# One kernel, a list order played in advance: a new account of DMAs, two weights loaded later, one more group turned, a longer finishing period

## The chip, the cores and the metric

The kernel runs on one core of a Trainium2 chip. Its time is the device time of one execution in microseconds (us); smaller is better. Three executions of the kernel before gave 932.15, 932.08 and 930.09 us, so the median is 932.08 us.

A core has five engines that take their own lists of instructions in order: TensorE (PE, matmuls; its weight loads are shown apart as PEld), VectorE (DVE), ScalarE (ACT), GpSimd (POOL) and SyncE (SP). In this kernel nearly every DMA is issued by SP. An instruction waits at the head of its list until the semaphores that it needs have come; what stands behind it waits too.

## The reference, cut to what matters

Four layers run one after the other on x of shape (8, 512, 256), all in float32. The first is a transformer block with a bias on the attention scores; it has nearly all the work.

```
x   = ln(src) * (1 + scale) + shift                 # scale, shift from an embedding of the step
q, k, v = x @ Wq + bq, x @ Wk + bk, x @ Wv + bv     # 16 heads of 16
scores  = q @ k.T / 4 + attention_bias              # bias: (8, 16, 512, 512) float32
scores  = where(mask, -inf, scores)
x   = x + softmax(scores) @ v @ Wo + bo
x   = x + gelu2((ln(x) * g2 + beta2) @ W1 + b1) @ W2 + b2   # 256 -> 1024 -> 256
x   = adapter(x, expert of the batch entry)         # 256 -> 64 -> 64 -> 256, residual, layer norm
x   = rotate(x, theta, phi)                         # pairs of columns
x   = adapter(x, expert of the batch entry)         # second set of weights
```

The bias is 128 MB and is read once. Everything else is small beside it.

## The kernel before, in words

**Units.** The attention is cut into 128 units. A unit is one batch entry, one group of four heads and one tile of 128 queries: it needs four bias tiles of 128x512, 256 KB each. Sixteen units make one batch entry. Within a batch entry the order is half (two query tiles), group, query tile; so eight units make one half.

**One unit (`attention`, L880 and after).** SP loads the four bias tiles (L898) into four of the 16 slots `BIAS`. POOL adds the mask, 0 or -1e30, to each (L902). PE makes the scores of four heads, which lie side by side in the rows of the array (L910; eight matmuls in the trace for one unit). DVE forms the negated sum of scores and bias and the minimum of each row (L922). ACT takes the exponential, less the row's maximum (L926). Then the 128x512 probabilities must be transposed for the product with v, and there are two ways:

- by PE: four transposes of 128x128 (L961) into one bank of PSUM, and one copy out by ACT or DVE (L682 in the profile, in the helper `evict`);
- "turned": DVE transposes 32x32 blocks (`nc.vector.transpose`, L937), and four DMAs issued by SP place the blocks (L946, pT<-tb). PE does nothing.

Where a group is turned, two of its four heads (`TURNED = 2`) take the second way. `turned_groups` (L361) says which groups: in the first batch entry only the last group, in the last batch entry all but the last group, in the others all four. For every second unit PE multiplies the probabilities of two query tiles with v (L987), transposes the result back (L1005), and DVE normalises it.

**Everything else.** `prepare(b)` makes normalised x, q, k and v of a batch entry, with its own loads of x and mask and of a broadcast modulation row (mod, L871), which waits until the kernel itself has written `ada_rows` (L486). `finish(b, ts)` does all that comes after attention for one half (two query tiles): the output product (L748), the feed-forward (L1043 into 1024 columns, L1052, L1055 and L1059 for the activation, L1068 back), two adapters (L1085, L1098, L748) and the rotation. `experts_matrices` fetches for each batch entry two small matrices chosen by an index that SP first reads from memory (L1210, then two DMAs at L1214). `late_weights` loads w1 and w2, 1024 KB each (L565, L567), and smaller ones.

**The order.** Nothing of this is written in the order in which it runs. Each piece is a `Task` with a cost, an engine, what it reads and writes, and a rank. `Plan.run` (L142) plays the list as a simulation on the host: whenever an engine is free it takes, among the tasks whose inputs are there and whose buffers are free, the one of the lowest rank. The order that comes out is the order in which instructions are emitted, and so the order of every engine's own list. The costs have no other effect; the chip runs the lists at its own pace. A DMA task costs SP its issue time; its data are taken to be there when a single counter, `queues`, has advanced by the task's `data`, plus 2.4 us. Any number of DMAs may be under way, and the counter starts at zero.

The ranks say how urgent a task is in units: bias loads of unit n have rank n - 2, the pieces of `finish` after unit n are spread by their PE cost from n + 2 to n + 11, for n from 110 on to n + 19 (L1278). For the last half the two query tiles are finished apart.

Of the kernel before, what the change touches and what calls it, by code (L numbers as in the profile page):

```python
# [20 lines left out]
B, S, D, H, HD, FF = 8, 512, 256, 16, 16, 1024  # L21
# [48 lines left out]


class Task:
    def __init__(self, costs, emit, rank, mode, at, data):
        self.costs, self.emit, self.rank, self.data = costs, emit, rank, data
        self.engine = None
        self.mode, self.at = mode, at
        self.waits, self.then, self.buffers = 0, [], []


class Plan:  # L80

    AFTER = {PE: 0.22, DVE: 0.14, ACT: 0.16, POOL: 0.12, DMA: 2.4}

    def __init__(self):
        self.tasks, self.written, self.read = [], {}, {}
        self.rank, self.stream = 0.0, None

    def __call__(self, engine, cost, emit, r=(), w=(), mode=None, at=0.0, data=0.0):  # L90


        if isinstance(engine, dict):
            task = Task(engine, emit, self.rank, mode, at, data)
        else:
            task = Task({engine: cost}, lambda e: emit(), self.rank, mode, at, data)
# [47 lines left out]
    def run(self, free_at):  # L144
        ready = {e: [] for e in free_at}
        mode = dict.fromkeys(free_at)
        events, order, seq = [], [], 0
        for n, t in enumerate(self.tasks):
            t.n = n
            if t.waits == 0:  # L150
                heapq.heappush(events, (t.at, seq, "ready", t))
                seq += 1
        for e, at in free_at.items():
            heapq.heappush(events, (at, seq, "free", e))
            seq += 1
        idle = set()
        now, queues = 0.0, 0.0
        while events:
            now, _, what, x = heapq.heappop(events)
            if what == "ready":  # L160
                for e in x.costs:

                    later = 1.0 if e == DVE and ACT in x.costs else 0.0
                    heapq.heappush(ready[e], (x.rank + later, x.n, x))
            elif what == "free":
                idle.add(x)
            elif what == "over":
                for b in x.buffers:
                    b.left -= 1
                    if b.left == 0:  # L170
                        b.home.free.append(b.slot)
            if events and events[0][0] == now:
                continue
            for e in [e for e in free_at if e in idle]:
                held, short = [], set()
                while ready[e]:
                    entry = heapq.heappop(ready[e])
                    t = entry[2]
                    if t.engine is not None:
                        continue  # L180
                    new = [b for b in t.buffers if b.slot is None]
                    wanted = {}
                    for b in new:
                        wanted[b.slots] = wanted.get(b.slots, 0) + 1
                    lacking = [
                        s for s, n in wanted.items()
                        if len(s.free) + (
                            len(s.lender.free) if s.lender and s.lender not in short else 0
                        ) < n
                    ]  # L190
                    if not lacking:
# [12 lines left out]
                if t.mode is not None and t.mode != mode[e]:  # L204
                    cost += 1.3 if e == ACT else 0.1
                    mode[e] = t.mode
                idle.discard(e)
                t.start, t.end = now, now + cost
                order.append(t)
                heapq.heappush(events, (t.end, seq, "free", e))  # L210
                seen = t.end
                if e == DMA:
                    queues = max(queues, now) + t.data
                    seen = max(seen, queues)
                seen += self.AFTER[e]
# [14 lines left out]
def conditioned_sequence_kernel(  # L230
# [129 lines left out]

    def turned_groups(b):  # L361

        return 3 if b == 0 else 0, NG - 1 if b == B - 1 else NG

    def rows_of(t, r, n):
        return t[:, r : r + 1, :].to_broadcast([P, n, D])
# [184 lines left out]
    def late_weights():  # L551
        wo_rows = w_o.rearrange("(c m e) n -> m e c n", c=NC, e=32)

        def load(rank, cost, data, emit, key):
            plan.rank = rank
            plan(DMA, cost, emit, [], [key], data=data)

        load(-1.5, 0.45, 0.8, lambda: nc.sync.dma_start(
            wv, w_v.rearrange("(c p) n -> p c n", p=P)), "wv")
# [1 line left out]
            bv_row, rows_in[R_BV * D : (R_BV + 1) * D].partition_broadcast(P)), "bv")  # L561
        load(2.5, 1.0, 1.0, lambda: [
            nc.sync.dma_start(wo[:, c], wo_rows[:, :HD, c]) for c in range(NC)
        ], "wo")
        load(1.1, 0.45, 3.0, lambda: nc.sync.dma_start(  # L565
            w1, w_1.rearrange("(c p) n -> p c n", p=P)), "w1")
        load(1.2, 0.45, 3.0, lambda: nc.sync.dma_start(  # L567
            w2, w_2.rearrange("(c p) n -> p c n", p=P)), "w2")
        load(2.6, 0.5, 0.5, lambda: nc.sync.dma_start(
            wd, down_w.rearrange("l (c p) a -> p l c a", p=P)), "wd")  # L570
# [4 lines left out]
    def rotations():  # L575
# [14 lines left out]
                )  # L590
            nc.sync.dma_start(cc.t[B : B + 1], rows_in[None, R_B2 * D : (R_B2 + 1) * D])

        plan(DMA, 1.0, load, [], [gb, (cc, "b2")], data=0.2)
        plan.rank = 2.5
        four = "p (g u v) -> p g u v"

# [26 lines left out]
        def store():  # L623
# [1 line left out]
            nc.sync.dma_start(turned_rows, cc.t[:B])  # L625

        plan(DMA, 0.7, store, [*((ab, u, v) for u in range(2) for v in (None, 0, 1)), (cc, "c")],
             ["rot_rows", "turned_rows"], data=0.2)

        def bias_rows():  # L630

# [7 lines left out]
            nc.sync.dma_start(wu[A1:K1, 1], turned_rows)  # L639

        plan.rank = 6.8
        plan(DMA, 1.6, bias_rows, ["turned_rows"], ["wu"], data=0.6)
        plan.rank = 7.0
        ps = Buffer(BG, lambda t: t[:, : NC * (B + 1)].rearrange("p (c b) -> p c b", c=NC))

# [112 lines left out]
    def prepare(b):  # L758
# [99 lines left out]
        plan(DMA, 1.8, turned_values, [(v_pad, t) for t in range(NT)], [v_turn], data=1.0)  # L858
# [29 lines left out]
    def attention(u, n):  # L888
# [60 lines left out]

        if turned:  # L950
            plan(DMA, 2.5, moved, [(tb, j) for j in range(turned)], [(pT, i)],
                 data=1.05 * TURNED)
        plan.rank = n + 0.0

        whole = "p (j k i q c) -> p j k i q c"
# [230 lines left out]
    def experts_matrices():  # L1186
# [19 lines left out]
        for b in range(B):  # L1206
            plan.rank = 2.7 + 0.55 * b

            def fetch(b=b):
                e = nc.sync.value_load(  # L1210
                    expert_i[:, b : b + 1], min_val=0, max_val=E - 1,
                )
                for l in range(2):
                    nc.sync.dma_start(  # L1214
                        raw.t[:, l, b, :],
                        experts[l].rearrange("(e p) a -> e p a", e=E)[bass.ds(e, 1)].rearrange(
                            "o p a -> (o p) a"),
                    )

            plan(DMA, 2.0, fetch, ["expert"], [(raw, b)], data=0.2)  # L1220

        def kept():
            nc.gpsimd.tensor_tensor(
# [43 lines left out]
    for n, u in enumerate(units):  # L1267
# [115 lines left out]
```

## Time and profile before

| | |
|---|---|
| three executions | 930.09 to 932.15 us, median 932.08 us |
| the profiled execution | 929.78 us |
| its span, first to last instruction | 927.8 us |
| PE busy | 893.6 us, 96% of the span |
| DVE, ACT, POOL busy | 788.3, 752.7, 754.0 us (85%, 81%, 81%) |
| DMA, mean over the core's 16 engines | 73.7% of the span for SP's queue; 216.48 MB at 233 GB/s |
| bias loads (L898) | 512 of 256 KB |
| transposes by PE (L961) | 1152 |
| block transposes by DVE (L937), DMAs that place them (L946) | 224, 448 |

How to read it. Busy time says how long an engine had an instruction in it. For PE this contains waiting inside the pipeline, so 96% does not mean that PE runs at its peak. More is told by the chain of waits (what released each step of the work that ended last) and by the busy times of each stretch of 25 us, because the kernel has a start, a long even middle and an end, and each has another limit. Where the profile puts an idle time down to "DMA bias<-in_bias", a bias tile had not landed. The granted clock of PE (1.00 is full speed) stands in the table of stretches too.

### The profile page before, as it was taken

To read this page: it belongs to the slowest core of one execution; us is meant where nothing else is said; L and a number is where in the kernel's file an instruction comes from. 1 tells how busy PE (TensorE), PEld (TensorE's weight loads), DVE (VectorE), ACT (ScalarE), POOL (GpSimd) and SP (SyncE) were. 2 spreads that over 40 slices of the span, in tenths; PEclk is the share of its full clock that TensorE was granted. 3 is DMA by queue.
4 is the path that set the end of the run, shared out by engine and by line. 5 is a ranking of instruction groups with operands and counts; after the bars stand their busy time and mean duration, and the time that the engine had idled before them with its cause. 6 is when DMAs were issued, how large, how long until landed. Compare 5 with 4: busy or idle time off the path is not lost.

```text
span 927.8 us, 21009 instructions
## 1 busy us (share of the span) xinstructions
PE 893.6 (96%) x6654; PEld 591.8 (64%) x6654; DVE 788.3 (85%) x2152; ACT 752.7 (81%) x1387; POOL 754.0 (81%) x843
## 2 busy tenths in 40 slices
PE   9989999999999999999999999999999999899994
PEld 7545766566666666667666666666666676566783
DVE  4557888988988989889998889989899899999666
ACT  5957869969898889969799697987989697998553
POOL 7589899987998878978798887989789788989132
PEclk9989999999999999999999999999999999999997
DMA  9578487787977879796966979877895978978000
GB/s 318 192 240 280 151 285 230 215 285 208 300 231 233 262 235 301 203 292 216 315 216 215 303 223 281 261 247 243 251 289 164 288 229 275 288 235 270 18 24 24
DMA packets 160913, 216.48 MB, mean 233 GB/s; under 512 B 18911, under 2 KB 91657, under 8 KB 160802
## 3 DMA queue, kind: packets, MB, share of 16 engines
q1 hardware_dynamic: 160758, 215.12, 73.7%
q8 instruction: 53, 0.87, 0.4%
q14 instruction: 58, 0.48, 0.2%
q10 hardware_dynamic: 44, 0.02, 0.0%
HBM read 149.89 MB, written 4.24 MB: 166 GB/s over the span
## 4 chain that ended last, share of the span: by engine, by line
PE 59%; ACT 10%; DMA 10%; DVE 9%; POOL 6%; issue 4%; SPq 2%; POOLq 0%; DVEq 0%; ACTq 0%
PE bank L910 10%; PE bank L1068 9%; PE bank L961 9%; PE bank L1043 9%; PE bank L987 8%; PE bank L748 4%; DMA bias<-in_bias 4%; PE bank L800 4%; POOL bias L902 3%; ACT bias L926 3%; DMA pT<-tb 2%; DVE bias L922 2%; PE bank L724 2%; ACT pT L682 2%; PE bank L838 1%
## 5 line engine op out<-in xcount | busy, mean ns | idle before, releaser
L902 POOL TENSOR_TENSOR bias<-bias,neg 128x512 f32<-128x512 f32 x512 | 580.1, 1161 | 81.6 <-DMA bias<-in_bias 63.7
L926 ACT ACTIVATE bias<-bias,low 128x512 f32<-128x512 f32 x512 | 344.8, 722 | 62.0 <-DVE low L922 61.2
L922 DVE CUSTOM_DVE_ANT_0 bias<-bank,bias 128x512 f32<-128x512 f32 x512 | 329.7, 684 | 48.3 <-PE bank L910 35.2
L961 PEld LDWEIGHTS bank<-shifted,bias 128*128 128x128 f32 x1152 | 129.0, 142 | 57.1 <-issue 21.6
L961 PE MATMUL bank<-shifted,bias 128*128 128x128 f32 x1152 | 159.3, 279 | 4.5 <-ACT pT L682 2.3
L937 DVE STREAM_TRANSPOSE tb<-bias 128x512 f32<-128x512 f32 x224 | 148.0, 691 | 11.1 <-DMA pT<-tb 8.6
L910 PE MATMUL bank<-kT,qz 32*128 32x512 f32 x1024 | 155.2, 645 | 2.0 <-DVE low L922 1.9
L682 ACT COPY pT<-bank 128x512 f32<-128x512 f32 x209 | 114.3, 588 | 36.1 <-PE bank L961 34.5
L1043 PE MATMUL bank<-hT,w 128*128 128x256 f32 (+1 forms) x544 | 127.1, 374 | 2.1 <-ACT pT L682 0.8
L987 PE MATMUL bank<-pT,v_pad 128*32 128x256 f32 x1152 | 123.0, 382 | 0.0
L1068 PE MATMUL bank<-w,gT 128*128 128x256 f32 x496 | 117.8, 384 | 0.1
L987 PE MATMUL bank<-pT,v_turn 128*32 128x256 f32 x896 | 107.6, 382 | 2.0 <-DMA pT<-tb 2.0
L1043 PEld LDWEIGHTS bank<-hT,w 128*128 128x128 f32 x544 | 94.2, 190 | 23.9 <-issue 4.0
L1068 PEld LDWEIGHTS bank<-w,gT 128*128 128x128 f32 x496 | 90.4, 190 | 26.8 <-issue 13.5
L987 PEld LDWEIGHTS bank<-pT,v_turn 128*32 128x32 f32 x896 | 48.0, 109 | 49.7 <-issue 5.3
L910 PEld LDWEIGHTS bank<-kT,qz 32*128 32x128 f32 x1024 | 44.0, 184 | 46.6 <-issue 26.8
L1055 POOL TENSOR_SCALAR sig<-sig 128x512 f32<-128x512 f32 (+1 forms) x68 | 40.5, 596 | 40.1 <-ACT sig L1052 35.0
L1052 ACT ACTIVATE sig<-bank,b1s 128x256 f32<-128x256 f32 (+1 forms) x136 | 55.0, 456 | 9.9 <-PE bank L1043 9.4
L1059 DVE SCALAR_TENSOR_TENSOR gT<-bank,cols,sig 128x256 f32<-128x256 f32 (+1 forms) x128 | 53.5, 464 | 10.5 <-POOL sig L1055 10.4
L987 PEld LDWEIGHTS bank<-pT,v_pad 128*32 128x32 f32 x1152 | 54.8, 109 | 7.9 <-issue 1.9
L690 DVE BATCH_NORM_STATS2 st<-res 128x6 f32<-128x256 f32 x128 | 52.3, 409 | 5.4 <-DMA res<-in_x 3.5
L682 DVE COPY pT<-bank 128x512 f32<-128x512 f32 x79 | 52.5, 682 | 3.8 <-PE bank L961 3.4
(142 smaller groups left out, 1156.3 us busy)
## 6 DMA issues: line engine op xcount, KB each, us to landing
bias<-in_bias SPq DMA_DIRECT2D x512, 256.0 KB
pT<-tb SPq DMA_DIRECT2D x448, 128.0 KB
out<-res SPq DMA_DIRECT2D x15, 256.0 KB
res<-in_x SPq DMA_DIRECT2D x7, 512.0 KB
v_turn<-v_pad SPq DMA_DIRECT2D x32, 68.0 KB
m<-in_mask SPq DMA_DIRECT2D x8, 256.0 KB
w<-in_w SPq DMA_DIRECT2D x2, 1024.0 KB
mod<-ada_rows SPq DMA_DIRECT2D x8, 256.0 KB
```

Source lines behind the costliest of these rows:

```text
L682: nc.scalar.copy(*pair()) if e == ACT else nc.vector.tensor_copy(*pair())), r, w)
L902: plan(POOL, 1.12, lambda j=j: nc.gpsimd.tensor_tensor(dif[j].t, dif[j].t, negs[qt].t, ALU.add), [negs[qt]], [dif[j]])
L910: nc.tensor.matmul(sc[j].t, qz.t[strip, par, c, qs], kT.t[strip, c, :], start=True, stop=True,)
L922: plan(DVE, 0.61, lambda j=j: nc.vector.tensor_tensor_reduce(dif[j].t, sc[j].t, dif[j].t, -1.0, 3.0e38, ALU.add, ALU.min, low.t[:, j : j + ...
L926: plan(ACT, 0.61, lambda j=j: nc.scalar.activation(dif[j].t, dif[j].t, AF.Exp, bias=low.t[:, j : j + 1], scale=-1.0), [(low, j)], [dif[j]] ...
L937: plan(DVE, 0.62, lambda j=j: nc.vector.transpose(tb.t.rearrange("p (m h k c) -> h p k m c", m=4, h=TURNED, k=NT)[j], dif[j].t.rearrange(" ...
L961: nc.tensor.transpose(ps.t[:, kc, :], dif[j].t[:, kc * P : (kc + 1) * P], ident)
L987: nc.tensor.matmul(pv.t[32 * j : 32 * j + 32, :], (v_turn if j < turned else v_pad).t[:, at : at + 32], pj, start=(kc == 0), stop=(kc == N ...
L1043: nc.tensor.matmul(ps.t[:, i, :w], w1[:, c, f * P : (f + 1) * P], hT.t[:, c, :w], start=(c == 0), stop=(c == NC - 1),)
L1052: plan(ACT, 0.155 + 0.1 * n, lambda i=i, f=f, ps=ps, sg=sg: nc.scalar.activation(sg.t[:, i, :w], ps.t[:, i, :w], AF.Tanh, bias=b1s[:, f : ...
L1059: plan(DVE, 0.14 + 0.13 * n, lambda i=i, f=f, ps=ps, sg=sg: nc.vector.scalar_tensor_tensor(gT.t[:, f, :w], ps.t[:, i, :w], cols[:, C_B1 + ...
L1068: nc.tensor.matmul(ps.t[:, i, :], gT.t[:, f, i * P : (i + 1) * P], w2[:, f, :], start=(f == 0), stop=(f == NF - 1),)
```

## The change

It touches the playing of the list, and four of its inputs.

1. **The account of DMAs in `Plan.run`.** A backlog of 9.0 us stands in front of the DMA engines at the start. At most eight DMAs are under way: a DMA is begun only when the eighth before it has landed, and until then SP counts as taken. A task says how many DMAs it issues (`many`). The data count as there 0.4 us earlier than by the counter before.
2. **w1 and w2** get ranks 3.1 and 4.1, where they had 1.1 and 1.2.
3. **`turned_groups`**: in the last batch entry all four groups are turned.
4. **The finishing period**: the half that ends with unit 103 is also spread to n + 19; it was spread to n + 11. (Units 111 and 119 were so before.)

```diff
     AFTER = {PE: 0.22, DVE: 0.14, ACT: 0.16, POOL: 0.12, DMA: 2.4}
+    BACKLOG = 9.0
+    FLIGHT = 8
...
-        now, queues = 0.0, 0.0
+        now, queues = 0.0, self.BACKLOG
+        landed = [self.BACKLOG + 1.5] * self.FLIGHT
...
                 idle.discard(e)
+                if e == DMA:
+                    begun = now
+                    for _ in range(t.many):
+                        begun = max(begun, landed[-self.FLIGHT]) + cost / t.many
+                        queues = max(queues, begun) + t.data / t.many
+                        landed.append(queues + 1.5)
+                    cost = begun - now
                 t.start, t.end = now, now + cost
...
                 if e == DMA:
-                    queues = max(queues, now) + t.data
-                    seen = max(seen, queues)
+                    seen = max(seen, queues - 0.4)
                 seen += self.AFTER[e]
...
     def turned_groups(b):
 
-        return 3 if b == 0 else 0, NG - 1 if b == B - 1 else NG
+        return (NG - 1 if b == 0 else 0), NG
...
-        load(1.1, 0.45, 3.0, lambda: nc.sync.dma_start(
+        load(3.1, 0.45, 3.0, lambda: nc.sync.dma_start(
             w1, w_1.rearrange("(c p) n -> p c n", p=P)), "w1")
-        load(1.2, 0.45, 3.0, lambda: nc.sync.dma_start(
+        load(4.1, 0.45, 3.0, lambda: nc.sync.dma_start(
             w2, w_2.rearrange("(c p) n -> p c n", p=P)), "w2")
...
-                plan.end(n + 2.0, n + (11.0 if n < 110 else 19.0))
+                plan.end(n + 2.0, n + (11.0 if n < 100 else 19.0))
```

The rest of the diff passes `many` along: 2 for wo, 3 for the rows of the rotation, 2 and 4 for their stores and the bias rows, 4 for the turned values and for the DMAs that place the turned blocks, 2 for an expert.

What it does to the lists. The instructions are the same but for the turned group: PE has 1120 transposes (L961) instead of 1152, DVE has 232 block transposes instead of 224, SP issues 464 DMAs at L946 instead of 448, and eight copies out of PSUM are gone. The order changes on every engine. SP's list at the start is the plainest: before, the issues after the first 16 bias tiles are w1, w2, three rows, wo, wd, the store of `ada_rows`, then the experts of four batch entries, and only then the four bias tiles of the fifth unit. After, they are the store of `ada_rows` (it stands ahead of the last four of the 16), three rows, the load of mod, and the four bias tiles of the fifth unit; then wo, wd and one pair of experts, two bias tiles, the four stores of the turned values, two bias tiles, w1, two pairs of experts, the sixth bias group and so on, with w2 and the other experts, two pairs at a time, between the bias tiles of the units that follow.

More of the change, by code (lines that the diff above doesn't have):

```diff
@@ L72, with __init__ @@
 class Task:
-    def __init__(self, costs, emit, rank, mode, at, data):
+    def __init__(self, costs, emit, rank, mode, at, data, many):
         self.costs, self.emit, self.rank, self.data = costs, emit, rank, data
         self.engine = None
-        self.mode, self.at = mode, at
+        self.mode, self.at, self.many = mode, at, many
         self.waits, self.then, self.buffers = 0, [], []
@@ L88, in __init__, with __call__ @@
         self.rank, self.stream = 0.0, None
-    def __call__(self, engine, cost, emit, r=(), w=(), mode=None, at=0.0, data=0.0):
+    def __call__(self, engine, cost, emit, r=(), w=(), mode=None, at=0.0, data=0.0, many=1):
         if isinstance(engine, dict):
-            task = Task(engine, emit, self.rank, mode, at, data)
+            task = Task(engine, emit, self.rank, mode, at, data, many)
         else:
-            task = Task({engine: cost}, lambda e: emit(), self.rank, mode, at, data)
+            task = Task({engine: cost}, lambda e: emit(), self.rank, mode, at, data, many)
         needs = []
@@ L552, in late_weights, with load @@
         wo_rows = w_o.rearrange("(c m e) n -> m e c n", c=NC, e=32)
-        def load(rank, cost, data, emit, key):
+        def load(rank, cost, data, emit, key, many=1):
             plan.rank = rank
-            plan(DMA, cost, emit, [], [key], data=data)
+            plan(DMA, cost, emit, [], [key], data=data, many=many)
         load(-1.5, 0.45, 0.8, lambda: nc.sync.dma_start(
@@ L563, in late_weights @@
             nc.sync.dma_start(wo[:, c], wo_rows[:, :HD, c]) for c in range(NC)
-        ], "wo")
-        load(1.1, 0.45, 3.0, lambda: nc.sync.dma_start(
+        ], "wo", many=NC)
+        load(3.1, 0.45, 3.0, lambda: nc.sync.dma_start(
             w1, w_1.rearrange("(c p) n -> p c n", p=P)), "w1")
-        load(1.2, 0.45, 3.0, lambda: nc.sync.dma_start(
+        load(4.1, 0.45, 3.0, lambda: nc.sync.dma_start(
             w2, w_2.rearrange("(c p) n -> p c n", p=P)), "w2")
@@ L591, in load @@
             nc.sync.dma_start(cc.t[B : B + 1], rows_in[None, R_B2 * D : (R_B2 + 1) * D])
-        plan(DMA, 1.0, load, [], [gb, (cc, "b2")], data=0.2)
+        plan(DMA, 1.0, load, [], [gb, (cc, "b2")], data=0.2, many=3)
         plan.rank = 2.5
@@ L627, in rotations @@
         plan(DMA, 0.7, store, [*((ab, u, v) for u in range(2) for v in (None, 0, 1)), (cc, "c")],
-             ["rot_rows", "turned_rows"], data=0.2)
+             ["rot_rows", "turned_rows"], data=0.2, many=2)
         def bias_rows():
@@ L641, in rotations @@
         plan.rank = 6.8
-        plan(DMA, 1.6, bias_rows, ["turned_rows"], ["wu"], data=0.6)
+        plan(DMA, 1.6, bias_rows, ["turned_rows"], ["wu"], data=0.6, many=4)
         plan.rank = 7.0
@@ L856, in turned_values @@
                 nc.sync.dma_start(to[m, :, :size], v_pad.t[32 * m : 32 * m + 32, :size])
-        plan(DMA, 1.8, turned_values, [(v_pad, t) for t in range(NT)], [v_turn], data=1.0)
+        plan(DMA, 1.8, turned_values, [(v_pad, t) for t in range(NT)], [v_turn], data=1.0, many=4)
         negs = [Buffer(NEG) for _ in range(NT)]
@@ L951, in attention @@
             plan(DMA, 2.5, moved, [(tb, j) for j in range(turned)], [(pT, i)],
-                 data=1.05 * TURNED)
+                 data=1.05 * TURNED, many=4)
         plan.rank = n + 0.0
@@ L1218, in fetch @@
                     )
-            plan(DMA, 2.0, fetch, ["expert"], [(raw, b)], data=0.2)
+            plan(DMA, 2.0, fetch, ["expert"], [(raw, b)], data=0.2, many=2)
         def kept():
```

## The prediction

> **What bounds the kernel now.** I read the table of 25 us stretches first, because one mean over the span mixes a start, a middle and an end. Columns: stretch, length, then PE, PEld, DVE, ACT, POOL busy (with counts), PE's granted clock, DMA share, GB/s.
>
> ```profile
> 0.00:25.00 25.00, 23.59 (x132) 17.80 (x136) 11.29 (x46) 14.95 (x31) 19.99 (x44) 1.00 0.96 323
> 25.00:50.00 25.00, 23.04 (x149) 13.30 (x142) 15.04 (x42) 22.18 (x45) 13.96 (x15) 0.98 0.54 168
> 50.00:75.00 25.00, 21.79 (x123) 12.19 (x121) 14.30 (x43) 13.45 (x25) 22.73 (x21) 0.82 0.80 258
> 75.00:100.00 25.00, 24.83 (x227) 15.52 (x230) 22.13 (x66) 20.16 (x35) 21.36 (x23) 1.00 0.77 255
> ...
> 875.00:900.00 25.00, 25.00 (x179) 21.34 (x168) 15.86 (x45) 11.88 (x34) 8.43 (x20) 1.00 0.07 22
> 900.00:925.00 25.00, 15.97 (x85) 11.14 (x83) 17.51 (x51) 9.47 (x26) 8.03 (x21) 0.82 0.05 17
> ```
>
> From 75 to 900 us PE is busy 23 to 25 of every 25 us: PE bounds the middle. Work taken from PE there is worth its full length, a stall removed elsewhere nothing. Between 25 and 75 us PE does half the instructions of the next stretch (123 against 227), at a lower clock, while the DMA engines are half idle. After 905 us there is a chain of small steps of the last query tile.
>
> The second view is the timeline of the start, on SP (its DMA issues), POOL and PE.
>
> ```profile
> 26.36 1.42 SPq L563 DMA_DIRECT2D wo<-in_w_o  x2
> 28.37 0.40 SPq L569 DMA_DIRECT2D wd<-in_down_w  x1
> 31.69 0.29 SPq L486 DMA_DIRECT2D ada_rows<-sig  x1
> 33.33 8.03 SPq L1214 DMA_DIRECT2D gT<-in_experts  x8
> 41.49 1.93 SPq L898 DMA_DIRECT2D bias<-in_bias  x4
> ```
>
> ```profile
> 18.62 13.43 POOL L902 TENSOR_TENSOR bias<-bias,neg 128x512 f32<-128x512 f32 x12
> ...
> 44.85 4.49 POOL L902 TENSOR_TENSOR bias<-bias,neg 128x512 f32<-128x512 f32 x4 [10.14 <-DMA bias<-in_bias]
> ```
>
> ```profile
> 46.79 5.41 PE L910 MATMUL bank<-kT,qz 32*128 32x512 f32 x8 [1.90 <-DVE low L922]
> 52.14 0.69 PE L1005 MATMUL bank<-shifted,pvs 128*128 128x128 f32 x2
> 52.62 4.80 PE L961 MATMUL bank<-shifted,bias 128*128 128x128 f32 x28
> ...
> 68.36 0.44 PE L1005 MATMUL bank<-shifted,pvs 128*128 128x128 f32 x2 [3.07 <-ACT pvs L682]
> ```
>
> The bias of the fifth unit is issued at 41.49, behind w1 and w2 and eight expert loads. POOL has nothing to do for 10.14 us; PE then needs 5.41 us for one unit's scores, which take 1.07 us elsewhere in the chain.
>
> How large is the stall? The PE groups from 44.9 to 75.0 us, at the lengths that the chain of waits gives them in the full stretches (scores of a unit 1.07, eight transposes 1.02, product with v 1.86, two matmuls of L800 0.86, L1005 0.22), are 16.1 us of work in 30.1 us: PE loses 14.0 us.
>
> **The change part by part.**
>
> *Order at the start (accounting of DMAs, w1 and w2).* In the new list the bias of the fifth unit stands behind the store of ada_rows, three rows and mod, ahead of wo, wd and all experts, and w1, w2 come later. Its slots are freed by the first transposes at PE (25.7 us). So it is issued at about 27 instead of 41.49 and lands (2.88 us in the chain) near 31, while POOL still works on the fourth unit, until 32.1, and then on four small rows until 34.7. The wait of 10.14 us goes.
>
> What is late next is the question. POOL's own work from the fifth to the eighth unit is 16 x 1.16 = 18.6 us, plus four rows of mod at 1.27 and one of 0.72: 24.4 us. Before, it began at 44.85 and the ninth unit began at 71.3, with 2.9 us of further waits. From 34.7 without any wait it ends at 59.1, so 12.2 us earlier. But the moved pieces now stand between the bias loads: four stores of the turned values (2.45 us of SP), w1 and w2 (1 MB each; at 369 GB/s, the rate from 20 to 30 us, 2.8 us), and experts, two batch entries at a time (2.0 us per entry by the 8.03 us row, 4.0 together). Following SP's new list with these lengths against POOL's, I get POOL waiting about 2.4 us for the sixth and seventh unit, 1.8 for the eighth and 1.5 for the ninth, so 5 to 6 us in all. An earlier store of ada_rows costs SP up to 2 us (its input is ready at 18.6, its place is reached at 16.7), hidden by loads still under way. Net shift at the ninth unit: -6.5; PE has slack for it (16.1 us of work). I add 1 us for the clock and take **-7.5**; bounds -14.0 (PE's whole loss) and +7 (second rival below).
>
> The clock: it was 0.50 from 50 to 54 us, and again from 70 to 72, after idle times of 1.90 and 3.07 us and the slow scores between.
>
> The Trainium skill, "TensorE: Matmul & The Clock Gate", section "HAM oscillation", gives as an abstract rule that PE should have no idle gaps above about 3.4 us. By that rule neither gap would slow the clock and only 5.0 us of gaps could come back. The row shows half clock after both, but matmuls that wait inside the pipeline may count as idle. My sum uses neither, since POOL sets the pace there.
>
> *One more turned group.* Two heads of four units: 8 x 4 = 32 transposes fewer on PE. In the chain at the end sixteen take 1.75 us, so 32 are 3.5 us (at 0.59 per four, the other row, 4.7).
>
> ```profile
> 863.15 1.75 PE bank L961 x16
> ...
> 870.21 1.75 PE bank L961 x16
> ```
>
> They lie between 815 and 875 us, where PE is full: **-3.5**. Eight copies (0.59 to 0.68 us) leave ACT and DVE, eight block transposes of 0.69 us come to DVE, 16 issues of 0.6 us to SP; from 850 on none is full (POOL 8 to 9 of 25 us, DMA share 0.28 and 0.07). What can be late is the placing DMA of the last unit: 2.1 to 5.2 us from issue to use in the chain of waits, plus DVE 1.4, SP 2.5 and DVE and ACT ahead of it (about 3), 9 to 12 us after the scores. In the new PE list the last product with v stands behind 16 us of work counted from the last scores. So it is covered; without cover it costs up to 3, and the gain shrinks to 0.5.
>
> *Finishing period of unit 103.* No instruction changes. By PE's list about 6 us of finishing work (priced as above) move from ahead of unit 112 to behind unit 120. PE is full on both sides: **0**, bounds -3 and +3. The first may come because less is left after the last product with v (32.5 instead of 35.0 us), the second because units there follow faster than POOL (4.65 us a unit) allows.
>
> *The middle.* The new account re-plays the whole list. Measured against work at the lengths above, every four units lose 0.7 to 5.0 us, 2.3 on average, 28 times. PE's new list has the same work ahead of the same unit within 0 to 5 us. I take **0**; scatter of about 0.8 us per group that is not the same in both lists gives sqrt(28) x 0.8 = 4 us either way.
>
> Sum for the profiled execution: 929.8 - 7.5 - 3.5 = 918.8. The median of the runs is 2.3 above that execution (932.08 against 929.78), so **921.1** as a median.
>
> **Rivals.**
>
> 1. *Only the turned group pays.* The start is late again for other reasons: the middle is PE's, but what PE lost at the start was also finishing work that isn't ready before unit 8. Then 929.8 - 3.5 = 926.3, median 928.6. For it: POOL has 22.7 of 25 us at 50 to 75. Against it: POOL's idle 10.14 us is plainly a DMA issued late.
> 2. *Slower: SP becomes a gate between units.* Three clusters of two experts (4.0 each), w1 and w2 (2.8 each) and the turned values (2.45) stand ahead of bias loads. If POOL has no stock and waits for each in full, that is 20.1 us against 13.1 removed (10.14 + 1.04 + 1.88): +7, less 3.5 for the turned group: median 935.6. It decides when the new waits exceed 16.6 us; slower by over 0.3% needs 19.4.
> 3. *The middle re-drawn badly*: +5, median 926; drawn well and a start near its bound: 911.
> 4. *The account does nothing* (same order, hence same time): excluded for the start, where the lists differ; for the middle it is my forecast.
>
> **Numbers.** My forecast 0.62; rival 1 0.13; rival 2 0.06; rival 3 bad 0.09, good 0.10. Range 911 to 931: it takes in rivals 1 and 3 and leaves out rival 2. A measurement of this kernel tells from no change what is over about 0.3%, 2.8 us: faster means below 929.3. Faster 0.85, same 0.09, slower 0.06.
>
> **What would show it.** POOL's 10 us wait gone, the wait for bias in 25 to 100 us down to some 6; the clock of 50 to 75 us near 1.00; the ninth unit's scores 6 to 8 us earlier; 1120 transposes; the last product with v about 11 us earlier, and the rest after it as long as before. I am wrong if PE's busy share between 75 and 900 falls, if POOL waits behind w1, w2 or experts for over 10 us, or if PE waits for pT<-tb at the end.

## The result, and the profile after

| | before | after |
|---|---|---|
| median of nine runs each, taken together | 931.9 us | 921.69 us (918.8 to 927.73) |
| ratio, 95% interval | 1 | 0.9905 (0.9889 to 0.9921) |
| profiled execution, span | 929.78, 927.8 us | 921.15, 918.9 us |
| PE busy | 893.6 us | 888.2 us |
| POOL's waits for bias from 25 to 100 us: sum, longest | 11.2, 10.1 us | 9.1, 2.6 us |

The change takes 8.9 us by the ratio, 10.2 by the medians; the forecast was 11.0 and 921.1 us. The median came out 0.6 us from the forecast; the gain by the ratio (interval 7.4 to 10.3 us) is somewhat smaller than forecast. The terms of the sum did not come out, and most of what follows is about them.

First the stretches of the kernel after, with the columns of the table in the prediction (the last stretch ends with the span, at 918.9):

```profile
25.00:50.00 25.00, 24.96 (x184) 16.25 (x184) 20.81 (x61) 24.80 (x51) 20.99 (x22) 1.00 0.57 181
50.00:75.00 25.00, 24.91 (x168) 13.63 (x168) 17.00 (x47) 18.14 (x32) 17.16 (x19) 0.86 0.71 222
75.00:100.00 25.00, 24.44 (x205) 16.52 (x203) 19.04 (x57) 18.25 (x33) 22.56 (x23) 1.00 0.93 310
875.00:900.00 25.00, 24.18 (x161) 21.06 (x160) 16.99 (x49) 12.55 (x37) 9.66 (x22) 1.00 0.08 22
900.00:925.00 25.00, 7.86 (x41) 4.36 (x39) 11.94 (x32) 6.25 (x16) 4.96 (x16) 0.77 0.07 22
```

Read the counts, not the busy time. From 25 to 75 us PE now runs 352 instructions where it ran 272, so the hole is about half filled; but from 50 to 75 it is "busy" for 24.91 of 25 us with 168 of them at clock 0.86, so part of this busy time is waiting inside its instructions. From 75 to 100 it does 205 where it did 227, a first sign that part of the gain is given back. POOL's timeline says what the waits have become:

```profile
32.63 3.40 POOL L911 TENSOR_TENSOR bias<-bias,neg 128x512 f32<-128x512 f32 x3
35.99 1.28 POOL L886 TENSOR_TENSOR res<-res,mod 128x512 f32<-128x512 f32 x1
37.22 4.53 POOL L911 TENSOR_TENSOR bias<-bias,neg 128x512 f32<-128x512 f32 x4
...
59.91 4.51 POOL L911 TENSOR_TENSOR bias<-bias,neg 128x512 f32<-128x512 f32 x4 [2.62 <-DMA bias<-in_bias]
65.73 2.27 POOL L911 TENSOR_TENSOR bias<-bias,neg 128x512 f32<-128x512 f32 x2 [1.31 <-DMA bias<-in_bias]
68.79 2.27 POOL L911 TENSOR_TENSOR bias<-bias,neg 128x512 f32<-128x512 f32 x2 [0.79 <-DMA bias<-in_bias]
...
74.10 2.27 POOL L911 TENSOR_TENSOR bias<-bias,neg 128x512 f32<-128x512 f32 x2 [2.14 <-DMA bias<-in_bias]
78.57 2.28 POOL L911 TENSOR_TENSOR bias<-bias,neg 128x512 f32<-128x512 f32 x2 [2.19 <-DMA bias<-in_bias]
```

One wait of 10.14 us has become five of 0.79 to 2.62, all from 57 us on. SP's list of the same time shows what the bias tiles stand behind: the experts, four DMAs (those of two batch entries) at a time, and further on the placing of turned blocks as well:

```profile
26.86 1.78 SPq L907 DMA_DIRECT2D bias<-in_bias  x4
...
53.08 3.06 SPq L1223 DMA_DIRECT2D gT<-in_experts  x4
56.24 2.56 SPq L907 DMA_DIRECT2D bias<-in_bias  x4
59.57 3.04 SPq L1223 DMA_DIRECT2D gT<-in_experts  x4
62.72 1.94 SPq L907 DMA_DIRECT2D bias<-in_bias  x4
64.77 2.64 SPq L955 DMA_DIRECT2D pT<-tb  x4
68.20 1.23 SPq L1223 DMA_DIRECT2D gT<-in_experts  x2
...
71.36 1.78 SPq L907 DMA_DIRECT2D bias<-in_bias  x4
```

The first wait (2.62) is for the bias of unit 7, the next two (2.10) for that of unit 8. The last two, 4.33 of the 9.1 us, are for that of unit 9, issued at 71.36; it stands behind the placing DMAs, one batch entry of experts and four small loads.

At the end, the chain of waits ends in the same kinds of steps as before, only earlier. Its last product with v and its last step, first in the kernel before, then after:

```profile
874.46 1.86 PE bank L987 x32
...
924.74 0.42 DVE res L1125
```

```profile
868.68 1.86 PE bank L996 x32
...
915.78 0.42 DVE res L1134
```

The last product with v comes 5.8 us earlier, and from there to the last step it takes 47.1 us where it took 50.3. So 5.8 us come from all that lies ahead of that product, and 3.2 from what lies behind it. The forecast had the whole gain ahead of it.

**Where the time lies.** Three marks divide the span: the time at which DVE takes up the scores of unit 20 and of unit 104 (counted from 0; the line that reads them, L922 before and L931 after), and the end. From each stretch I take away the PE work that the kernel's list puts there, at the lengths that the prediction used. What is left is what PE loses there, in us. All kernels are in one table; each row is one profiled execution. Only differences between rows count, since the amounts depend on the lengths taken.

| kernel | first scores of unit 8, at | start to unit 20 | 20 to 104 | 104 to end | last product with v to end of span |
|---|---|---|---|---|---|
| before | 78.2 | 39.4 | 39.8 | 27.4 | 53.4 |
| account alone | 70.8 | 36.7 | 43.3 | 27.5 | 53.4 |
| weights alone | 75.2 | 36.3 | 40.5 | 30.0 | 53.2 |
| turned alone | 75.8 | 36.9 | 41.5 | 29.3 | 53.6 |
| period alone | 79.0 | 40.1 | 40.2 | 29.7 | 53.8 |
| turned and period | 79.3 | 40.8 | 39.4 | 28.1 | 50.4 |
| after | 66.9 | 33.4 | 42.0 | 25.8 | 50.3 |
| after, old account | 75.9 | 37.1 | 41.6 | 30.8 | 50.8 |
| after, old ranks of w1 and w2 | 70.5 | 36.1 | 40.9 | 26.9 | 50.8 |
| after, group not turned | 67.2 | 32.8 | 44.4 | 28.3 | 53.5 |
| after, old period | 66.0 | 32.8 | 43.3 | 32.3 | 51.9 |
| after, no limit of DMAs | 68.6 | 26.7 | 44.6 | 26.0 | 51.0 |
| after, AFTER of DMA 2.6 | 66.2 | 33.5 | 45.0 | 24.5 | 50.9 |
| after, experts later | 64.1 | 31.7 | 42.5 | 29.1 | 51.2 |

How far may one row be trusted? "Turned alone", "period alone" and "turned and period" have the same order of instructions as the kernel before up to unit 107 or later. Yet they reach unit 20 at 151.9, 155.2 and 155.9 us against 154.4, and unit 104 at 722.0, 723.8 and 723.8 against 722.7. So one profile of one list scatters by 2 us or so either way, and a difference of that size between two rows says nothing. The last column is steadier.

### The profile page after: what moved, and what is told of

Read it like the earlier page. It is cut to its first block, busy times and chain, and to the rows that moved or that the text cites. A ratio compares the mean times of both kernels' runs of the same rounds, so it can differ in the third digit from the quotient of the medians.

```text
span 918.9 us, 20978 instructions
## 1 busy us (share of the span) xinstructions
PE 888.2 (97%) x6622; PEld 587.5 (64%) x6622; DVE 788.6 (86%) x2157; ACT 753.5 (82%) x1382; POOL 752.8 (82%) x843
## 3 DMA queue, kind: packets, MB, share of 16 engines
q1 hardware_dynamic: 163062, 217.22, 75.2%
## 4 chain that ended last, share of the span: by engine, by line
PE 63%; ACT 15%; DVE 10%; DMA 5%; issue 3%; POOL 2%; SPq 1%; DVEq 0%; POOLq 0%; ACTq 0%
PE bank L919 10%; PE bank L1077 10%; PE bank L970 9%; PE bank L1052 9%; PE bank L996 9%; ACT bias L935 5%; PE bank L809 4%; PE bank L757 3%; DVE bias L931 3%; DMA bias<-in_bias 2%; PE bank L847 2%; PE bank L733 2%; ACT pT L691 2%; DMA pT<-tb 2%; PE bank L409 1%
## 5 line engine op out<-in xcount | busy, mean ns | idle before, releaser
L935 ACT ACTIVATE bias<-bias,low 128x512 f32<-128x512 f32 x512 | 347.9, 724 | 69.0 <-DVE low L931 68.6
L931 DVE CUSTOM_DVE_ANT_0 bias<-bank,bias 128x512 f32<-128x512 f32 x512 | 330.2, 683 | 50.3 <-PE bank L919 42.3
L970 PEld LDWEIGHTS bank<-shifted,bias 128*128 128x128 f32 x1120 | 126.0, 142 | 60.8 <-issue 20.0
L946 DVE STREAM_TRANSPOSE tb<-bias 128x512 f32<-128x512 f32 x232 | 152.9, 690 | 10.8 <-DMA pT<-tb 9.1
L919 PE MATMUL bank<-kT,qz 32*128 32x512 f32 x1024 | 151.7, 640 | 0.1
L691 ACT COPY pT<-bank 128x512 f32<-128x512 f32 x213 | 117.0, 586 | 21.2 <-PE bank L970 19.8
L996 PE MATMUL bank<-pT,v_turn 128*32 128x256 f32 x928 | 111.4, 382 | 4.6 <-DMA bias<-in_bias 2.1
L996 PEld LDWEIGHTS bank<-pT,v_turn 128*32 128x32 f32 x928 | 49.7, 109 | 54.6 <-ACT bias L935 6.6
L1064 POOL TENSOR_SCALAR sig<-sig 128x512 f32<-128x512 f32 (+1 forms) x68 | 40.2, 593 | 39.8 <-ACT sig L1061 34.8
L691 DVE COPY pT<-bank 128x512 f32<-128x512 f32 x67 | 44.8, 681 | 4.7 <-PE bank L970 4.7
```

The costliest lines, as they stand in the source:

```text
L691: nc.scalar.copy(*pair()) if e == ACT else nc.vector.tensor_copy(*pair())), r, w)
L919: nc.tensor.matmul(sc[j].t, qz.t[strip, par, c, qs], kT.t[strip, c, :], start=True, stop=True,)
L931: plan(DVE, 0.61, lambda j=j: nc.vector.tensor_tensor_reduce(dif[j].t, sc[j].t, dif[j].t, -1.0, 3.0e38, ALU.add, ALU.min, low.t[:, j : j + ...
L935: plan(ACT, 0.61, lambda j=j: nc.scalar.activation(dif[j].t, dif[j].t, AF.Exp, bias=low.t[:, j : j + 1], scale=-1.0), [(low, j)], [dif[j]] ...
L946: plan(DVE, 0.62, lambda j=j: nc.vector.transpose(tb.t.rearrange("p (m h k c) -> h p k m c", m=4, h=TURNED, k=NT)[j], dif[j].t.rearrange(" ...
L970: nc.tensor.transpose(ps.t[:, kc, :], dif[j].t[:, kc * P : (kc + 1) * P], ident)
```

## The experiments

The theory on trial was the sum of the prediction: the start pays 7.5 us and stays paid, the turned group 3.5, the period nothing. The rivals were that only the turned group pays, or that the start's gain comes from one of its two parts alone. All ratios below are to the kernel before, on the same chip.

### One part at a time, from before

**The account alone**: all of part 1 of the diff, with the old ranks, groups and period.

> The kernel before with the new account of DMAs alone; w1 and w2 keep their old ranks, so they stand ahead of the fifth unit's bias, but the experts stand behind it. Theory (SP's order at the start is what pays, and above all the place of the experts): POOL's wait of 10.1 us falls below 4 us, the first score of unit 20 comes 4 to 6 us earlier than the 154.4 us of before, and the time is 4 to 6 us shorter (-0.4 to -0.7%). Rival (the 2 MB of w1 and w2 in front of the bias are what delays it): the wait stays at 6 us or more and the time moves by less than 2 us.

Measured: 929.18 us, ratio 0.9965 (0.9942 to 0.9988), so -3.3 us. POOL's 10 us wait is gone; the longest for bias in this stretch is

```profile
44.91 1.16 POOL L911 TENSOR_TENSOR bias<-bias,neg 128x512 f32<-128x512 f32 x1 [3.59 <-DMA bias<-in_bias]
```

Unit 8 starts 7.4 us earlier, unit 20 2.7 us earlier (4 to 6 were expected), unit 104 not at all (723.5 against 722.7). This execution is no shorter than the profiled one of before (930.55 against 929.78 us), so its marks can't say where the 3.3 us of the times lie.

**The weights alone.**

```diff
-        load(1.1, 0.45, 3.0, lambda: nc.sync.dma_start(
+        load(3.1, 0.45, 3.0, lambda: nc.sync.dma_start(
...
-        load(1.2, 0.45, 3.0, lambda: nc.sync.dma_start(
+        load(4.1, 0.45, 3.0, lambda: nc.sync.dma_start(
```

> The kernel before with the new ranks of w1 and w2 alone. In this list w1, w2 and four batch entries of experts still stand ahead of the fifth unit's bias, only the order among them is another. Theory: POOL's wait stays at 8 to 10 us and the time moves by less than 2 us. Rival (the weights are what pays): the wait falls below 5 us and the time is 5 us or more shorter.

Measured: 928.36 us, ratio 0.9958 (0.9936 to 0.9979), -3.9 us. I had thought that the account's place for the experts makes the start, and that the weights bring less than 2 us; that falls. The rival asked for a wait below 5 us and a gain of 5 us or more, and falls too. It is not a clean start either. POOL still waits 6.50 us before the bias of the fifth unit, which SP issues at 36.43 instead of 41.49. The profile names a transpose at PE as what ended this wait. For the wait of 10.10 us in "period alone", whose list is there the one of before, it also names an instruction of PE, so the name does not rule out the bias load. PE waits 6.66 us once, where its longest wait from 25 to 100 us was 3.1 before. POOL's and PE's lines:

```profile
41.33 4.51 POOL L902 TENSOR_TENSOR bias<-bias,neg 128x512 f32<-128x512 f32 x4 [6.50 <-PE bank L961]
```

```profile
65.03 0.69 PE L1005 MATMUL bank<-shifted,pvs 128*128 128x128 f32 x2 [6.66 <-ACT pvs L682]
```

**The turned group alone**, and **the finishing period alone**:

```diff
-        return 3 if b == 0 else 0, NG - 1 if b == B - 1 else NG
+        return (NG - 1 if b == 0 else 0), NG
```

> The kernel before with the last group of the last batch entry turned and nothing else. Theory: 32 transposes less on a PE that is full, so 3.5 us (0.4%) shorter, start and middle as before, and no wait of PE for pT<-tb above 1 us after 850 us. Rival (the last placing DMA is late): PE waits 2 to 3 us for pT<-tb near the last product with v, and the time moves by less than 1 us.

```diff
-                plan.end(n + 2.0, n + (11.0 if n < 110 else 19.0))
+                plan.end(n + 2.0, n + (11.0 if n < 100 else 19.0))
```

> The kernel before with the longer period for unit 103 alone. Theory: the same work in another order on a full PE, within 1.5 us of before. Rival (the trace of after gains 5.2 us from unit 104 to the end, more than the 3.5 of the turned group, and the longer period is the rest): 1.5 to 3 us shorter, with the last product with v some 3 to 6 us earlier.

Measured: 930.02 us, 0.998 (0.9952 to 1.0008) for the group, so -1.9 us with anything from -4.5 to +0.7 possible; 930.1 us, 0.9967 (0.9946 to 0.9988) for the period, -3.1 us (by the medians 1.9). The period alone is faster than before beyond its interval, though no instruction is gone and though its one profiled execution (932.94) was slower than before's. The last product with v was to come 3 to 6 us earlier by the rival; in that execution it comes at 877.51 instead of 874.46. The two together:

> The kernel before with the turned group and the longer period, and nothing of the start. Theory (account and weights are two ways to the same gain at the start, together about 3.7 us; turned group and period make the rest): 5 us (0.5%) shorter than before, with the starts of units up to 100 as before and the last unit 5 us earlier. Rival (the start is worth the 7.5 us of the prediction and the end pays only with it): less than 2 us shorter.

Measured: 926.94 us, 0.994 (0.9921 to 0.996), -5.6 us. That is more than the 3.5 of the prediction. Expected was also that the last unit starts 5 us earlier; it does not (861.5 us, before 861.0), and what this profile gains lies behind the last product with v. The difference to the full change, 0.9940 against 0.9905, is about 3.3 us (about 1 to 6 by the two intervals, which only touch): this is what account and weights add to the other two.

### All but one part, from after

The edits are the reverse of those above.

> The changed kernel with the old account of DMAs; weights, turned group and period stay new. Its list at the start is the one of before but for w1 and w2, which stand between the experts: four batch entries of experts are ahead of the fifth unit's bias. Theory (the account makes the start): POOL waits 8 to 10 us again and the time is 926 to 929 us, the turned group's 3.5 us and little else being left of the gain of 10. Rival (weights and account each do half): 924 or less.

> The changed kernel with the old ranks of w1 and w2, which then stand ahead of the fifth unit's bias, while the experts stay behind it. Theory: 2 MB more in front of the bias cost 5.7 us of transfer at 369 GB/s, most of it while POOL still has the fourth unit, and nothing stands in the way of later bias loads any more: within 2 us of the changed kernel, 920 to 924 us. Rival (the weights matter as much as the experts): 926 us or more.

> The changed kernel with the last group of the last batch entry transposed by PE as before. Theory: 32 transposes more on a full PE, 3.5 us longer than the changed kernel, 924 to 926 us. Rival (the group is hidden anyway, the end being a chain of its own): within 1 us of the changed kernel.

> The changed kernel with the old period for unit 103. Theory: within 1.5 us of the changed kernel. Rival (the period is worth what the end gained beyond the turned group): 1.5 to 3 us longer, 923 to 925 us.

| without | median, us | ratio (95%) | to after's 0.9905, us |
|---|---|---|---|
| account | 924.78 | 0.9907 (0.9889 to 0.9925) | 0.2 |
| weights | 923.94 | 0.9908 (0.9891 to 0.9924) | 0.3 |
| turned group | 927.54 | 0.9933 (0.9915 to 0.9951) | 2.6 |
| period | 926.89 | 0.9925 (0.9907 to 0.9943) | 1.9 |

By the two intervals that go into it, a number of the last column is good to about 2 us either way; only that of the group stands clear of zero. Account and weights stand in for each other, as far as that allows: either alone is worth 3.3 to 3.9 us, the second one 0.2 to 0.3. In the profiles the second does seem to move the start (36 to 37 us of loss with one of them, 33.4 with both), but that gain isn't found in the times. Without the account POOL waits 7.20 us for the fifth unit's bias, a little less than the 8 to 10 expected, and yet the ratio is the one of after: the expectation that the account makes the start falls. Without the weights the time is within 2 us of after, as expected; the group came out at 2.6 of the expected 3.5; for the period the rival (1.5 to 3 us) holds.

The last column of the large table shows where a part of what the group and the period bring lies. From the last product with v to the end it is 53.2 to 53.8 us in every kernel without the turned group, with or without the period; 53.6 with the group but without the period; 51.9 with the group in the new list but the old period; and 50.3 to 51.2 in all seven kernels with both. The lists say the same: PE's work behind that product is 35.1 us without the group, 34.2 and 33.3 with it and the old period, and 32.5 with both. So 2.6 us less work behind that product go with some 3 us less time, and the whole of it takes both edits (in the new list the group alone has 1.6 of it, 53.5 to 51.9). What the moved work costs ahead of the product can't be read: the losses from unit 104 to the end differ by up to 6 us from profile to profile. By the times it costs less there than it saves.

### What in the account pays

The account has two main parts, the backlog at the start and the limit of eight. Here the limit is taken away, and the backlog stays:

```diff
-    FLIGHT = 8
+    FLIGHT = 1000
```

> The changed kernel whose account allows 1000 DMAs under way instead of 8; the backlog of 9 us stays. In its list most experts stand between the bias loads of the fifth and sixth unit again. Theory (the limit of eight is not what pays in the middle, and the gain at the start is the same with any order that has some bias ahead of the experts): 920 to 925 us, within the scatter of a re-drawn list. Rival (knowing the limit matters through the whole list): 926 us or more, with the loss growing evenly from unit 20 to unit 100.

Measured: 915.8 us (912.64 to 916.8), ratio **0.9814** (0.9784 to 0.9844). Both expectations were wrong: it is faster than both kernels, by 0.9814/0.9905 = 0.991 of after, 8 to 9 us (each compared with before, not directly with each other). Its stretches from 50 to 100 us:

```profile
50.00:75.00 25.00, 25.00 (x202) 14.90 (x201) 21.51 (x61) 20.02 (x36) 24.92 (x22) 1.00 0.86 266
75.00:100.00 25.00, 24.26 (x236) 16.05 (x235) 21.07 (x64) 20.25 (x38) 23.73 (x27) 1.00 0.91 298
```

POOL is busy for 24.92 of 25 us where it was busy for 17.16, PE does 202 instructions and then 236 where it did 168 and 205, and the clock stays at 1.00. SP's issue of eight bias tiles in a row, and POOL's use of them:

```profile
54.08 4.31 SPq L907 DMA_DIRECT2D bias<-in_bias  x8
```

```profile
60.33 14.59 POOL L911 TENSOR_TENSOR bias<-bias,neg 128x512 f32<-128x512 f32 x13
75.13 1.16 POOL L911 TENSOR_TENSOR bias<-bias,neg 128x512 f32<-128x512 f32 x1 [0.22 <-DMA bias<-in_bias]
```

In this list eight bias tiles come before the next experts, where after has four. POOL does thirteen tiles in a row without a wait, and its waits for bias in 25 to 100 us shrink from 9.1 to 0.6. Unit 8 is 1.7 us later than in after, with 2.0 us more work ahead of it, but unit 20 is 8.1 us earlier (140.4 against 148.5): from unit 8 to unit 20 PE loses 5.1 us, where it loses 11.5 in after, and unit 104 is still 6.7 us earlier (712.3 against 719.0). So the limit of eight isn't what pays, and with it the list gets worse. Which moved piece does it isn't isolated: other loads move too. The experts, for one, come earlier: 14 of their 16 DMAs are issued by 53 us, where after issues the last six from 59.57 on.

**Experts later.** If what remains in after is the waiting behind pairs of experts, they might be spread:

```diff
-            plan.rank = 2.7 + 0.55 * b
+            plan.rank = 3.5 + 1.0 * b
```

> The changed kernel with the experts' loads spread out, one batch entry per unit (rank 3.5 + b instead of 2.7 + 0.55 b). SP then issues at most one batch entry of experts (2 us) ahead of a unit's bias, where it was two. Theory (POOL's waits of 9 us between 56 and 80 us and PE's half clock from 67 to 74 us come from the pairs): POOL waits less than 5 us for bias there, no half clock before 100 us, unit 20 starts 2 to 4 us earlier than in the changed kernel, and the time is 1 to 3 us shorter, since the middle gives part of a head start back. Rival (the start is no longer what bounds): unit 20 moves, the time stays within 1 us or gets longer.

Measured: 923.35 us, 0.9912 (0.9879 to 0.9945): no gain over after. Unit 8 does start 2.8 us earlier than in after, unit 20 1.8 us earlier, but now PE itself waits:

```profile
74.12 0.64 PE L996 MATMUL bank<-pT,v_turn 128*32 128x256 f32 x2 [3.16 <-DMA gT<-in_experts]
```

The profile names an expert's DMA, but a product with v reads no expert. It reads the blocks that the placing DMAs issued from 67.07 to 69.59 bring, and these are the likelier releaser. POOL still waits 6.4 us for bias (up to 2.39 at once), where less than 5 was expected, and half clock is still there, from 73.4 to 76.8. Note the direction: here the experts come later, in the kernel without the limit they come earlier. So this run does not say whether their place alone made that kernel faster.

**How much a list's wander is worth.** The constant of a DMA's end is changed by 0.2 us, so that the list is drawn again with nothing meant by it:

```diff
-    AFTER = {PE: 0.22, DVE: 0.14, ACT: 0.16, POOL: 0.12, DMA: 2.4}
+    AFTER = {PE: 0.22, DVE: 0.14, ACT: 0.16, POOL: 0.12, DMA: 2.6}
```

> The changed kernel with one input of the playing nudged: data count as there 2.6 us after the account's end of transfer instead of 2.4. Every list is re-ordered in the middle, nothing is changed on purpose. This sizes the scatter that re-playing a list brings. Theory (scatter of 4 us, as the prediction put it): within 4 us of the changed kernel, and the distance between the two at equal units wanders by 2 to 4 us in the middle. Rival (the middle is the same whatever the order): within 1 us, and an even distance.

Measured: 923.76 us, 0.9905 (0.9877 to 0.9933), the ratio of after. Between the marks it moves, 45.0 instead of 42.0 us lost in the middle and 24.5 instead of 25.8 at the end, and the sum is the same within the interval. This is one sample of the scatter; the list without the limit, drawn again for another reason, is 8 to 9 us away.

## Why the prediction was right in the sum and wrong in its terms

**The mechanism at the start: right.** "It is issued at about 27": 26.86. The wait of 10.14 us is gone; the longest for bias is 2.62. What is late next is what the prediction named, bias tiles behind pairs of experts, though not for the units it named: 4.7 us of waits up to the ninth unit instead of "5 to 6", none of them for the sixth and seventh, and 4.3 more for the tenth, where the working had stopped.

**"Net shift at the ninth unit: -6.5 ... I take -7.5": the step that failed.** The shift itself was near. POOL begins the ninth unit (unit 8) at 65.73 instead of 71.32, 5.6 us earlier; DVE takes up its scores 11.3 us earlier, since they no longer come late from PE (62.91 instead of 76.86). But it was no gain yet. With the same work ahead of the unit in both lists, or counted against it, after is 11.3 us ahead at unit 8, 7.5 at unit 12, 6.9 at unit 16, 6.0 at unit 20 and 3.8 at unit 104, and by the times the two parts of the start add 3.3 us to the other two. The working stopped at the ninth unit and took the shift there for the gain. It did not ask whether POOL's and SP's lists behind it could hold the pace, and they did not: POOL waits 0.79 to 2.19 us before every two bias tiles, begins unit 12 at 90.91 instead of 92.25, only 1.3 us earlier, and from unit 8 to unit 12 PE loses 6.7 us instead of 2.9. Rival 1 had nothing left of the start, for another reason; the 3.3 us lie between it and the forecast.

The half clock of that time is not what takes the gain back. "After, old period" has the order of after up to 740 us, and its profiled execution kept the full clock there:

```profile
50.00:75.00 25.00, 24.91 (x192) 13.79 (x190) 18.15 (x51) 19.81 (x35) 18.13 (x21) 1.00 0.76 232
```

Yet from unit 8 to unit 12 it takes 29.0 us, where after takes 28.7, and it reaches unit 20 at 147.9 against 148.5. The loss is there without the half clock, and the 1 us that the prediction added for the clock is not seen either: 0.6 us lies within the scatter.

**"The clock of 50 to 75 us near 1.00": wrong.** It was 0.86 in this execution, with half clock from 67.0 to 73.9 us. The prediction had also read the pieces of before too short: they last from 49.0 to 55.8 and from 69.5 to 72.9 us, and the first begins inside the slow scores that start at 46.79.

**The middle, "0; scatter 4 us": its size holds, the sign is open.** After loses 42.0 us there, 39.8 before. The three lists with the start of after (after, group not turned, old period) lose 43.2 on average, the four with the order of before 40.2, so by these averages the middle gave back 3.0 us. Lists by the new account lost 40.9 to 45.0, by the old one 39.4 to 41.6. With 2 us of scatter per profile that is a hint, not a finding.

**The turned group, -3.5: a little high.** 32 transposes are gone:

```profile
L970 PE MATMUL bank<-shifted,bias 128*128 128x128 f32 x1120 | 157.9, 279 | 7.6 <-DVE gT L1068 3.5
L946 DVE STREAM_TRANSPOSE tb<-bias 128x512 f32<-128x512 f32 x232 | 152.9, 690 | 10.8 <-DMA pT<-tb 9.1
```

It measured 1.9 us alone (interval -0.7 to 4.5) and 2.6 within the rest. By the 1.02 us per eight transposes that the prediction took for the start, the term would have been 4.1, further off. That the placing DMA is covered was right: after 800 us PE's matmuls never wait for pT<-tb, whose DMAs there land 2.6 to 4.5 us after their issue.

**The finishing period, "0, bounds -3 and +3": at its bound.** It measured 3.1 us alone and 1.9 within the rest. The prediction had the reason for its lower bound, "less is left after the last product with v", and had even the two amounts (35.0 and 32.5 us), and yet took 0, since PE is full on both sides, so that work would cost ahead what it saves behind. What it saves behind is there (53.6 to 50.4 us when the period is added to the turned group); what it costs ahead didn't show in the times. Accordingly "the rest after it as long as before" was wrong by 3 us, and "about 11 us earlier" for the product itself was 5.8. What the period alone gains is not in that column (53.8); its place is not found.

So the start was overrated by about 4 us and the end underrated by about 2, and half of the error cancelled. That the median was met to 0.6 us is luck in part: for the profiled execution the forecast was 918.8 and 921.15 was measured, 2.4 us more, and the 2.3 us that were added for the median of before are only 0.5 in after (921.69 against 921.15). Rival 2 (SP as a gate) did not occur in the sum, but its mechanism, bias that stands behind other loads in SP's list, is what remains in after.

**What stays open.** Which moved load makes the list without the limit better; what costs the rest of the early start between units 20 and 104, if the scatter leaves anything to explain; where the period alone pays.

## What to carry to other kernels

Follow a removed stall through the queues until their stocks are full again, before you take the shift at the first place for the gain: here 11.3 us at unit 8 were 6.0 at unit 20 and about 3.3 in the time. Cost separately what lies behind the last heavy step, since work moved from there to ahead of it can pay even where no instruction goes. A planner's model that is closer to the machine doesn't have to give a better list, so vary its constants one at a time and time what comes out: the limit of eight cost 8 to 9 us here.

## What the runs showed of the hardware

**PE's clock is halved while PE counts as busy.** In after PE has no idle gap over 0.6 us from 25 to 100 us, and none over 0.1 us before 80 us, and yet the clock is 0.50 from 67.0 to 73.9. What goes ahead is a unit's scores that wait inside the pipeline, 3.51 us instead of 1.14 (PE's timeline of the kernel after):

```profile
62.91 3.51 PE L919 MATMUL bank<-kT,qz 32*128 32x512 f32 x8
...
66.94 1.92 PE L970 MATMUL bank<-shifted,bias 128*128 128x128 f32 x8
```

The eight transposes behind it take 1.92 us, against 1.09 at full clock in the kernel without the limit, which has no such stretch at all before the tail. In "after, old period", with the same order of instructions there, the scores at this place take 2.38 us and the clock stays at 1.00. Only the sequence was seen; that the waiting inside the scores is the cause wasn't tried by itself. The Trainium skill, "TensorE: Matmul & The Clock Gate", section "HAM oscillation", has idle gaps above about 3.4 us as the abstract rule; no idle gap of that length stands ahead of this stretch, so a look at gaps alone would have missed it.

**Half clock comes in pieces of 3.4 and 6.8 us ahead of the tail, and not in every execution of a list.** Before has one of 6.8 us at 49.0 and one of 3.4 us at 69.5. Of the three kernels with its order there, two have the same pair (49.7 and 70.2; 50.2 and 70.6), and "turned alone" has only the first. It reaches unit 20 2.5 us earlier, which is part of the scatter of one list. Of the three kernels with the order of after at the start, after and "group not turned" have the piece at 67.0 us, "old period" has none.
